# Projections of queries and keys on packed columns, placed by DMA, with a quarter of the adds on GpSimd

## The chip, the cores and the metric

The kernel runs on one NeuronCore of a Trainium2 chip. Its engines work side by side, each with a queue of its own: TensorE (PE, matmuls and transposes; PEld is its weight load), VectorE (DVE), ScalarE (ACT), GpSimd (POOL) and SyncE (SP, which here only issues DMAs). ACT and POOL can issue DMAs too. The metric is the device time of one execution in microseconds (us). A second, profiled execution gives the trace that the profile is read from.

## The reference

One transformer block in float32 on `x` of 4096 tokens by 256 features: a mixture of experts, attention, and the same mixture again.

```python
x = x + 0.5 * ffn(layernorm(x))
x = x + attention(layernorm(x))
x = x + 0.5 * ffn(layernorm(x))
```

`ffn` sends each token to 4 of 32 experts, adds their results with the routing weights, and adds a shared expert. `attention` has 16 heads of 16 features: `qkv = layernorm(x) @ qkv_w.T + qkv_b`, softmax of the scaled scores over all 4096 keys, times the values, and an output projection. The change concerns the adding up of the first mixture's results and the projections of queries and keys.

## The kernel before

**Order of the stages.** `first_front` normalizes and routes all tokens of the first mixture, clears the buffer `xg` and scatters the rows into it. `layer.experts` runs the experts and scatters their results into `ys`. `projections` adds up each token's results, normalizes, and makes queries, keys and values. `attention` runs scores, softmax and values, with the second mixture's front woven in; then come the second experts and a last loop that adds up and stores. The engines named in `ORDERED` (PE, ACT, DVE, SP) run the stage in the order of the program text; GpSimd's order is the framework's. DMAs issued on ACT or SP start in the order of those queues.

**Projections, block by block.** The stage has eight blocks (`NQB`) of 512 tokens (`QB`), four tiles of 128 each (`QT`). `fetch` loads the five rows of results per token of a tile, `y`, on SP; six such buffers exist, so a tile's load is asked for when the add of the tile six before it is done. `begin(c)` makes a block's rows:

- `add_up` (L763): per tile four DVE instructions (L765), each multiplying one expert's row by its weight `wk` and adding it to the sum; the first adds to the shared expert's row.
- `normalize` (L136): statistics (L141, L142) of the four tiles, an inverse root in some small steps (L144 to L157), then `xn` (L167), all on DVE.
- GpSimd adds the output projection's bias to `xt` (L910) and stores it to `x1` (L913) for attention.

A block's loop (L979 to L990) then goes: `turned` transposes the rows on PE (L177) and ACT copies them to `xT` (L180); `queries_or_keys(c, 0)`; `begin(c + 1)`, so that DVE makes the next block's rows meanwhile; `queries_or_keys(c, 1)`; `norms` of the queries; `values` (PE L961, DVE L969); `norms` of the keys; and a DVE reduction that sums `xT` over the block's tokens (L990).

**Layout of queries and keys.** Each head takes 32 rows (`HP`): 16 of data (`HD`), one row that is constant, and 15 rows of zeros. Four heads make one group of 128 rows, so 16 heads make four groups (`NG`). The weights `wqkv` come in this padded form, and each group costs one 128x512 product over two slices of the features (two matmuls at L922; the trace holds two records of each). ACT adds the bias twice per group: once as a plain copy (L935), into `kT` for keys and into a buffer `q` that ACT's queue stores to `qd` in DRAM for queries (L937), and once squared (L939). `norms` sums the squares by head with `of_head2`, four matmuls of 32 columns (L947), and DVE takes their maximum (L954).

**After the loop** the mean of the keys comes from the sums and the weights (L998 to L1025), then a bound on the scores and a shift for the queries (to L1044). A flag is read by all engines (L1343), and attention starts with a load of the first queries from `qd` (L1152).

**Loads at the stage's start** (L873 to L889), all on ACT's queue: `wqk_sb` (1 MB in pieces of 4 KB), `wv_sb` (two DMAs, in pieces of 64 bytes, one piece per head), `bv_sb` and `bproj_sb`.

Of the kernel before, what the change touches and what calls it, by code (L numbers as in the profile page):

```python
# [9 lines left out]
F32 = mybir.dt.float32  # L10
# [49 lines left out]
def kernel(  # L60
# [122 lines left out]
    class Layer:  # L183
# [573 lines left out]
        def finished(self, pool, t, xt):  # L757
# [2 lines left out]
            nc.sync.dma_start(y[:], by_token[:, t, :, :])  # L760
            self.add_up(y, t, xt)

        def add_up(self, y, t, xt):  # L763
            for k in range(K):
                nc.vector.scalar_tensor_tensor(  # L765
                    xt,
                    y[:, k, :],
                    self.wk[:, t, k : k + 1],
                    y[:, K, :] if k == 0 else xt,
                    ALU.mult,  # L770
                    ALU.add,
                )

    def first_front(layer, keep):
        n = layer.n
        with (
            tc.tile_pool(name="front", bufs=2) as pool,
            tc.tile_pool(name="ps_f", bufs=8, space=PSUM) as pm,
            tc.manual_schedule(engines=ORDERED),
        ):  # L780
            rows = 8
            zero = pool.tile([P, rows * RW], F32, name="zero", bufs=1)
            nc.vector.memset(zero[:], 0.0)
            nch = layer.nch
            xts = [
                pool.tile([P, n, D], F32, tag="x", name="xt", bufs=nch) for _ in range(nch)
            ]

            def load(ch, m):
                for i in range(0, n, m):  # L790
                    t = ch * n + i
                    nc.sync.dma_start(xts[ch][:, i : i + m, :], x_in[:, t : t + m, :])

            load(0, 2)
            load(1, n)


            xg = xgs[0]
            for e in range(E):
                nc.sync.dma_start(  # L800
                    xg[e * S0 + LOW : (e + 1) * S0, :].rearrange("(p r) d -> p (r d)", p=P),
                    zero[:, : (S0 - LOW) // P * RW],
                )
            for r in range(E * S0, CLEARED, rows * P):
                nc.sync.dma_start(
                    xg[r : r + rows * P, :].rearrange("(p r) d -> p (r d)", p=P), zero[:]
                )
            for ch in range(2, nch):
                load(ch, n)

            routes = [layer.route(ch, xts[ch], pool, pm) for ch in range(nch)]
            xTs = []

            def go_on(ch, pieces):
                for _ in range(pieces):
                    next(routes[ch])

            turns = NC * n // QT

            def norm(ch):  # L820
                go_on(ch, 2)
                xTs.append(layer.xT)

            def halves():
                for h in range(NT // QT):
                    ch, i = divmod(h, n // QT)
                    yield layer.shared_half(
                        xts[ch][:, i * QT : (i + 1) * QT, :],
                        xTs[ch][:, :, i * QB : (i + 1) * QB],
                        h * QT,  # L830
                        pool,
                        pm,
                    )

            half = halves()
            norm(0)
            go_on(0, turns)
            norm(1)
            for ch in range(nch):
                go_on(ch, 1)  # L840
                if ch + 1 < nch:
                    go_on(ch + 1, turns)
                go_on(ch, 2)
                between = next(half) if ch > 0 else iter(())
                next(between, None)
                go_on(ch, 3)
                next(between, None)
                if ch + 2 < nch:
                    norm(ch + 2)
                next(between, None)  # L850
            flag = layer.low(keep)

            late = iter(())
            for it in half:
                next(it)
                next(it)
                next(late, None)
                late = it
            next(late, None)
        return flag  # L860

    def projections(layer, side):
# [4 lines left out]
        with (  # L867
# [1 line left out]
            tc.tile_pool(name="ps_p", bufs=8, space=PSUM) as pm,  # L869
            tc.manual_schedule(engines=ORDERED),  # L870
        ):
            wqk_sb = pool.tile([P, NC, 2 * NG * P], F32, name="wqk_sb", bufs=1)
            nc.scalar.dma_start(  # L873
                wqk_sb[:], wqkv[:, : 2 * NG * P].rearrange("(c p) e -> p c e", p=P)
            )
            wv_sb = pool.tile([P, NC, NH, HD], F32, name="wv_sb", bufs=1)
            for c in range(NC):
                nc.scalar.dma_start(
# [20 lines left out]
            def begin(c):  # L899

                xt = pool.tile([P, QT, D], F32, tag="x", name="xt")
                for i in range(QT):
                    layer.add_up(ys_of.pop(c * QT + i), c * QT + i, xt[:, i, :])
                    if c * QT + i + 6 < NT:
                        ys_of[c * QT + i + 6] = fetch(c * QT + i + 6)
                xn = pool.tile([P, QT, D], F32, tag="xn", name="xn")
                rows = [xn[:, i, :] for i in range(QT)]
                for _ in normalize(pool, xt, rows, QT):
                    pass
                nc.gpsimd.tensor_tensor(  # L910
                    xt[:], xt[:], bproj_sb[:].unsqueeze(1).to_broadcast([P, QT, D]), ALU.add
                )
                nc.gpsimd.dma_start(x1_at[:, c * QT : (c + 1) * QT, :], xt[:])  # L913
                return rows

            def queries_or_keys(c, i, xT):

                squares = []
                for g in range(NG):
                    ps = pm.tile([P, QB], F32, tag="m", name="qk_ps")  # L920
                    for cc in range(NC):
                        nc.tensor.matmul(  # L922
                            ps[:],
                            wqk_sb[:, cc, (i * NG + g) * P : (i * NG + g + 1) * P],
                            xT[:, cc, :],
                            start=(cc == 0),
                            stop=(cc == NC - 1),
                        )
                    bias = bqk_sb[:, i * NG + g : i * NG + g + 1]
                    if i == 0:  # L930
                        q = pool.tile([P, QB], F32, tag="q", name="q", bufs=3)
                        part = q[:]
                    else:
                        part = kT[:, g, c * QB : (c + 1) * QB]
                    nc.scalar.activation(part, ps[:], AF.Identity, bias=bias)  # L935
                    if i == 0:
                        nc.scalar.dma_start(qd[c, g], part)  # L937
                    sq = pool.tile([P, QB], F32, tag="sq", name="sq", bufs=2 * NG - 1)
                    nc.scalar.activation(sq[:], ps[:], AF.Square, bias=bias)  # L939
                    squares.append(sq)  # L940
                return squares
# [1 line left out]
            def norms(c, i, squares):  # L943

                ps = pm.tile([P, QB], F32, tag="m", name="sq_ps")
                for g in range(NG):
                    nc.tensor.matmul(  # L947
                        ps[g * HP : (g + 1) * HP, :],
                        of_head2,
                        squares[g][:],  # L950
                        start=True,
                        stop=True,
                    )
# [24 lines left out]
            rows = begin(0)  # L978
            for c in range(NQB):  # L979
                xT = pool.tile([P, NC, QB], F32, tag="xT", name="xT")  # L980
                for _ in turned(pm, rows, QT, xT, nc.scalar.copy):
                    pass
                q2 = queries_or_keys(c, 0, xT)
                if c + 1 < NQB:
# [2 lines left out]
                norms(c, 0, q2)  # L987
                values(c, xT)
                norms(c, 1, k2)
                nc.vector.tensor_reduce(sums[:, :, c : c + 1], xT[:], AX.X, ALU.add)  # L990

# [6 lines left out]
            mean_in = small.tile([P, NC], F32, name="mean_in")  # L1000
            nc.vector.tensor_reduce(mean_in[:], sums[:], AX.X, ALU.add)
            nc.vector.tensor_scalar(mean_in[:], mean_in[:], 1.0 / T, None, ALU.mult)
            ps = pm.tile([P, NG], F32, tag="m", name="kmean_ps")
            for g in range(NG):
                for cc in range(NC):
                    nc.tensor.matmul(
                        ps[:, g : g + 1],
                        wqk_sb[:, cc, (NG + g) * P : (NG + g + 1) * P],
                        mean_in[:, cc : cc + 1],
                        start=(cc == 0),  # L1010
                        stop=(cc == NC - 1),
                    )
            mean = small.tile([P, NG], F32, name="mean")
            nc.vector.tensor_add(mean[:], ps[:], bqk_sb[:, NG:])
            nc.vector.tensor_mul(mean[:], mean[:], mean[:])
            ps = pm.tile([P, 1], F32, tag="m", name="mean_ps")
            for g in range(NG):
                nc.tensor.matmul(
                    ps[g * HP : (g + 1) * HP, :],
                    of_head2,  # L1020
                    mean[:, g : g + 1],
                    start=True,
                    stop=True,
                )
# [279 lines left out]
    for base, step, sign in ((0, -HP, 1), (HD - 1, HP, -1)):  # L1304
# [6 lines left out]
            base=base,  # L1311
            channel_multiplier=sign,
        )
    of_head2 = of_head[:].rearrange("p j r -> p (j r)")

    rows = const.tile([P, HG], F32, name="rows")
    nc.gpsimd.memset(rows[:], 1.0 / SCALE)
# [106 lines left out]
```

## Time and profile before

| What | us |
|---|---|
| Median of 3 runs (3371.22 to 3374.43) | 3372.26 |
| The profiled execution | 3374.66 |
| Span of its trace, first to last instruction | 3372.8 |
| TensorE busy in the span | 3072.7 (91%) |
| ScalarE busy | 2334.9 (69%) |
| VectorE busy | 975.3 (29%) |
| GpSimd busy | 616.0 (18%) |
| First load of results in the projections | 502.0 |
| First matmul of attention | 711.8 |

The page gives busy times over the whole span, a picture of the span in 40 slices, the DMA queues, the chain of work that ended last, and groups of instructions with what each waited for. Since the shares are means over stages with different limits, the stage that the change touches has to be read by itself: the timeline (start, length, engine, line, tile) and the busy time by stretches show which engine never rests there. A group's row reads: line, engine, operation, result and inputs, shapes, count, then busy us and mean ns of one, then the idle time before and what ended it.

### The profile page before, as it was taken

The page shows a single profiled execution, that of the slowest core. Times are in us where ns is not written, and L with a number is a line of the kernel's source. Part 1 is how long each engine was busy: PE and PEld are TensorE (multiplying, and loading weights), DVE is VectorE, ACT ScalarE, POOL GpSimd, SP SyncE. Part 2 cuts the span into 40 slices and gives each one's busy share as a digit, 9 for nine tenths or more (in the row PEclk, how much of TensorE's full clock was granted, in tenths as well). Part 3 has the DMA queues.
Part 4 walks back from the last instruction along what each step waited for, and adds up shares of the span by engine and source line. Part 5 has one row for each costly group of instructions (what it writes and reads, how often), then busy time and mean ns, then how long its engine had stood idle before and what let it go on. Part 6 is the DMA issues. An engine that isn't in the chain of part 4 may idle for free.

```text
span 3372.8 us, 50148 instructions
## 1 busy us (share of the span) xinstructions
PE 3072.7 (91%) x20183; PEld 1066.8 (32%) x20183; DVE 975.3 (29%) x2837; ACT 2334.9 (69%) x3753; POOL 616.0 (18%) x644
## 2 busy tenths in 40 slices
PE   4589977989999999999999999999999999959990
PEld 3356653422222222222222222222222222226660
DVE  6744437810112103201211210220121131044447
ACT  2112224569999898898999989889989998912220
POOL 2756661100001000100100010010010001025661
PEclk9799998989999999999999999999999999969995
DMA  6347756441300000000000010000000000017767
GB/s 236 118 182 244 247 189 242 153 135 56 100 4 20 26 7 4 27 20 4 30 20 4 13 33 4 7 27 20 4 30 20 4 6 31 1 64 238 254 204 315
DMA packets 130352, 282.20 MB, mean 84 GB/s; under 512 B 23472, under 2 KB 70192, under 8 KB 129712
## 3 DMA queue, kind: packets, MB, share of 16 engines
q1 hardware_dynamic: 82976, 165.84, 14.6%
q0 software_dynamic: 31872, 97.56, 7.9%
q10 hardware_dynamic: 15248, 15.38, 1.3%
q8 instruction: 163, 2.67, 0.3%
q14 instruction: 93, 0.76, 0.1%
HBM read 146.64 MB, written 132.06 MB: 83 GB/s over the span
## 4 chain that ended last, share of the span: by engine, by line
PE 70%; DVE 3%; issue 2%; DMA 2%; POOL 1%; ACT 0%; DVEq 0%; POOLq 0%; SPq 0%
PE banks L1170 33%; PE banks L1188 30%; PE banks L375 2%; DMA ys<-yb,toi 2%; PE h L718 2%; DVE xt L765 1%; POOL ys L748 1%; PE banks L1260 1%; PE banks L395 1%; PE o L740 1%; PE banks L233 1%; PE xbt_ps L692 0%; PE banks L177 0%; POOL wb L663 0%; DVE hT L729 0%
## 5 line engine op out<-in xcount | busy, mean ns | idle before, releaser
L1180 ACT ACTIVATE ex<-banks 128x512 f32<-128x512 f32 (+1 forms) x3223 | 2055.7, 714 | 164.7 <-PE banks L1170 129.1
L1170 PE MATMUL banks<-q,kT 32*128 32x512 f32 x8192 | 1177.6, 641 | 12.4 <-DVE q L1157 11.1
L1188 PE MATMUL banks<-ex,v 128*17 128x512 f32 x8192 | 1078.9, 598 | 0.0
L350 POOL DMA_INDIRECT xg<-xr,sidx x256 | 248.2, 969 | 2282.3 <-DVE beyond L343 2163.4
L1170 PEld LDWEIGHTS banks<-q,kT 32*128 32x128 f32 x8192 | 327.4, 183 | 847.4 <-ACT ex L1180 704.5
L1188 PEld LDWEIGHTS banks<-ex,v 128*17 128x17 f32 x8192 | 136.1, 95 | 777.5 <-issue 776.5
L1208 DVE COPY o<-banks 128x512 f32<-128x512 f32 x32 | 22.1, 691 | 1185.4 <-PE banks L1188 647.2
L748 POOL DMA_INDIRECT ys<-yb,toi x304 | 293.0, 964 | 177.3 <-DVE yb L746 94.8
L718 PE MATMUL h<-xT,w 128*128 128x512 f32 x512 | 236.0, 604 | 0.0
L744 ACT COPY yb<-o 128x512 f32<-128x512 f32 x64 | 37.5, 586 | 178.8 <-PE o L740 153.0
L740 PE MATMUL o<-w,hT 128*128 128x256 f32 x512 | 126.7, 392 | 34.2 <-DVE hT L729 34.2
L698 ACT COPY xT<-xbt_ps 128x512 f32<-128x512 f32 (+1 forms) x112 | 50.6, 452 | 126.4 <-PE xbt_ps L692 124.8
L727 ACT ACTIVATE s<-h 128x512 f32<-128x512 f32 (+1 forms) x112 | 51.5, 460 | 107.0 <-PE h L718 105.4
L718 PEld LDWEIGHTS h<-xT,w 128*128 128x128 f32 x512 | 95.2, 196 | 95.2 <-issue 95.2
L922 PE MATMUL qk_ps<-xT,wqk_sb 128*128 128x512 f32 x256 | 113.5, 602 | 1.7 <-ACT xT L180 1.7
L740 PEld LDWEIGHTS o<-w,hT 128*128 128x128 f32 x512 | 95.4, 194 | 55.1 <-DVE hT L729 36.9
L1211 DVE RECIPROCAL den<-den 128x512 f32<-128x512 f32 x32 | 107.3, 3353 | 1.1
L765 DVE SCALAR_TENSOR_TENSOR xt<-y,wk,xt 128x256 f32<-128x256 f32 x192 | 95.1, 495 | 6.9
L729 DVE TENSOR_TENSOR hT<-s,h 128x512 f32<-128x512 f32 (+1 forms) x112 | 57.8, 516 | 74.9 <-PE h L718 71.7
L375 PE MATMUL banks<-xT,ws_sb 128*128 128x512 f32 x128 | 68.9, 664 | 8.6 <-DVE u L385 6.5
L692 PE MATMUL xbt_ps<-ident,xb 128*128 128x128 f32 x512 | 69.6, 282 | 7.7 <-DMA xb<-xg 7.7
L443 PE MATMUL so<-ws_sb,shT 128*128 128x256 f32 x128 | 36.2, 441 | 43.5 <-DVE shT L437 28.9
(215 smaller groups left out, 1781.2 us busy)
## 6 DMA issues: line engine op xcount, KB each, us to landing
y<-ys SPq DMA_DIRECT2D x64, 640.0 KB, 6.9
xb<-xg SPq DMA_DIRECT2D x64, 528.0 KB, 5.7
w<-in_wexp_dram SPq DMA_DIRECT2D x64, 384.0 KB, 3.4
xg<-zeros SPq DMA_DIRECT2D x152, 132.0 KB, 2.3
xg<-zero SPq DMA_DIRECT2D x32, 264.0 KB, 4.3
qd<-q ACTq DMA_DIRECT2D x32, 256.0 KB, 5.5
q<-qd SPq DMA_DIRECT2D x32, 256.0 KB, 2.6
xbb<-xg SPq DMA_DIRECT2D x48, 132.0 KB, 3.7
```

Source lines behind the costliest of these rows:

```text
L350: ins = nc.gpsimd.indirect_dma_start(out=self.xg[:], out_offset=bass.IndirectOffsetOnAxis(ap=self.sidx[:, t0 + t, k : k + 1], axis=0), in_ ...
L375: nc.tensor.matmul(ps[:], ws13_sb[:, c, h0 : h0 + P], xT[:, c, i0 * P : (i0 + QT) * P], start=(c == 0), stop=(c == NC - 1),)
L692: nc.tensor.transpose(tp[:, i * P : (i + 1) * P], xb[:, i, c * P : (c + 1) * P], ident[:])
L718: nc.tensor.matmul(ps[:, : n * P], w[:, (j * NC + c) * H : (j * NC + c + 1) * H], xT[:, c, : n * P], start=(c == 0), stop=(c == NC - 1),)
L740: nc.tensor.matmul(o[:, i, :], hT[:, (i0 + i) * P : (i0 + i + 1) * P], w2, start=True, stop=True)
L748: ins = nc.gpsimd.indirect_dma_start(out=ys[:], out_offset=bass.IndirectOffsetOnAxis(ap=b["toi"][:, i : i + 1], axis=0), in_=yb[:, i, :], ...
L765: nc.vector.scalar_tensor_tensor(xt, y[:, k, :], self.wk[:, t, k : k + 1], y[:, K, :] if k == 0 else xt, ALU.mult, ALU.add,)
L922: nc.tensor.matmul(ps[:], wqk_sb[:, cc, (i * NG + g) * P : (i * NG + g + 1) * P], xT[:, cc, :], start=(cc == 0), stop=(cc == NC - 1),)
L1170: nc.tensor.matmul(pm.all[:, banks[j], :], kT[rows, g, t * P : (t + 1) * P], q[rows, :], start=True, stop=True,)
L1180: nc.scalar.activation(ex[:, i : i + n, :], pm.all[:, k : k + n, :], AF.Exp, scale=SCALE)
L1188: nc.tensor.matmul(acc[j * HP : j * HP + HV, :], v[:, t, g * HG + j, :], ex[:, j, :], start=(t == 0), stop=(t == NT - 1),)
L1211: nc.vector.reciprocal(den[:], den[:])
```

## The change

Two groups of heads share one set of 128 columns: the 16 rows that were padding for the first hold the second's data, so queries take two products instead of four, and keys likewise.

- **Weights.** `wqk_sb` is loaded by 16 DMAs on ACT's queue instead of one, each leaving out the padding (pieces of 64 bytes). The bias is brought to the same layout by six small DVE instructions.
- **Queries.** The padding rows of `qd` are cleared once, by 16 DMAs on SP in `first_front`, behind the loads of `x`. ACT adds the bias into a buffer `q`, and eight DMAs of 16 rows each, on SP, put its parts where attention expects them.
- **Keys.** ACT first fills the block's part of `kT` (the constant row and zeros), then eight DMAs per product place the 16-row parts in it, on SP too.
- **Squares and norms.** Two squares instead of four, and two matmuls of 64 columns with a new constant `of_half`, made by three GpSimd instructions. The mean of the keys follows the layout.
- **Sums.** ACT's copies to `xT` give the sums over tokens as they go; DVE's reduction L990 is dropped.
- **Adds.** The fourth tile of each block is added up on GpSimd by `add_up_aside`, four instructions; the other three stay on DVE. The last loop of the kernel keeps `add_up`.

```diff
+        def add_up_aside(self, y, t, xt):
+            w = self.wk[:, t, :].unsqueeze(2).to_broadcast([P, K, D])
+            nc.gpsimd.tensor_tensor(y[:, 0:K, :], y[:, 0:K, :], w, ALU.mult)
+            nc.gpsimd.tensor_tensor(y[:, 0:2, :], y[:, 0:2, :], y[:, 2:4, :], ALU.add)
+            nc.gpsimd.tensor_tensor(y[:, 0, :], y[:, 0, :], y[:, 1, :], ALU.add)
+            nc.gpsimd.tensor_tensor(xt, y[:, 0, :], y[:, K, :], ALU.add)
...
+            for g in range(NG):
+                for j in range(HG):
+                    nc.sync.dma_start(
+                        qd[:, g, j * HP + HD : (j + 1) * HP, :].rearrange("b r q -> r b q"),
+                        zero[:HP - HD, :QB].unsqueeze(1).to_broadcast([HP - HD, NQB, QB]),
+                    )
...
-            nc.scalar.dma_start(
-                wqk_sb[:], wqkv[:, : 2 * NG * P].rearrange("(c p) e -> p c e", p=P)
-            )
+            for cc in range(NC):
+                for a in range(2):
+                    for g in range(NG):
+                        h, i = divmod(g, 2)
+                        first_col = (a * NG + g) * P
+                        nc.scalar.dma_start(
+                            wqk_sb[:, cc, a, h].rearrange("p (j i d) -> p i j d", j=HG, i=2)[:, i],
+                            wqkv[
+                                cc * P : (cc + 1) * P, first_col : first_col + P
+                            ].rearrange("p (j r) -> p j r", j=HG)[:, :, :HD],
+                        )
...
-                    layer.add_up(ys_of.pop(c * QT + i), c * QT + i, xt[:, i, :])
+                    t = c * QT + i
+                    add = layer.add_up if i < QT - 1 else layer.add_up_aside
+                    add(ys_of.pop(t), t, xt[:, i, :])
...
+                cols = slice(c * QB, (c + 1) * QB)
+                if i == 1:
+                    nc.scalar.activation(
+                        kT[:, :, cols],
+                        zeros[:, 0:1].unsqueeze(2).to_broadcast([P, NG, QB]),
+                        AF.Identity,
+                        bias=one_row[:],
+                    )
                 squares = []
-                for g in range(NG):
+                for h in range(NG // 2):
...
-                            wqk_sb[:, cc, (i * NG + g) * P : (i * NG + g + 1) * P],
+                            wqk_sb[:, cc, i, h],
...
-                    nc.scalar.activation(part, ps[:], AF.Identity, bias=bias)
-                    if i == 0:
-                        nc.scalar.dma_start(qd[c, g], part)
-                    sq = pool.tile([P, QB], F32, tag="sq", name="sq", bufs=2 * NG - 1)
+                    bias = bias_sb[:, i, h : h + 1]
+                    part = pool.tile([P, QB], F32, tag="q", name="q", bufs=4)
+                    nc.scalar.activation(part[:], ps[:], AF.Identity, bias=bias)
+                    for r in range(0, P, HD):
+                        j, g = r // HP, 2 * h + r % HP // HD
+                        rows = slice(j * HP, j * HP + HD)
+                        if i == 0:
+                            nc.sync.dma_start(qd[c, g, rows, :], part[r : r + HD, :])
+                        else:
+                            nc.sync.dma_start(kT[rows, g, cols], part[r : r + HD, :])
+                    sq = pool.tile([P, QB], F32, tag="sq", name="sq", bufs=NG)
...
-                for g in range(NG):
+                for h in range(NG // 2):
                     nc.tensor.matmul(
-                        ps[g * HP : (g + 1) * HP, :],
-                        of_head2,
-                        squares[g][:],
+                        ps[h * 2 * HP : (h + 1) * 2 * HP, :],
+                        of_half,
+                        squares[h][:],
...
-                for _ in turned(pm, rows, QT, xT, nc.scalar.copy):
+                sums_of = iter([sums[:, cc, c : c + 1] for cc in range(NC)])
+                for _ in turned(
+                    pm,
+                    rows,
+                    QT,
+                    xT,
+                    lambda out, ps: nc.scalar.activation(
+                        out, ps, AF.Identity, accum_out=next(sums_of)
+                    ),
+                ):
...
-                nc.vector.tensor_reduce(sums[:, :, c : c + 1], xT[:], AX.X, ALU.add)
```

## The prediction

> **What bounds the kernel now.** I read the page from the top: the run without a profile and the profiled one agree (3372.26 us median of 3; 3374.66 us for the profiled execution, whose span is 3372.8, so 1.9 us lie around the span). The chain of work that ended last gives PE 70%, nearly all of it attention (L1170, L1188), which the change does not touch. So I went to the stage it does touch: the projections, from 502 us (the first load of results) to 711.8 us (the first attention matmul). First its costliest group on the page, then the timeline of one of its eight blocks, PE and DVE together:
>
> ```profile
> L922 PE MATMUL qk_ps<-xT,wqk_sb 128*128 128x512 f32 x256 | 113.5, 602 | 1.7 <-ACT xT L180 1.7
> ...
> 652.45 1.09 PE L177 MATMUL tp<-ident,xn 128*128 128x128 f32 x8
> 654.40 0.48 DVE L765 SCALAR_TENSOR_TENSOR xt<-y,wk 128x256 f32<-128x256 f32 x1
> 662.23 0.42 DVE L141 BATCH_NORM_STATS2 st<-xt 128x6 f32<-128x256 f32 x1
> 666.86 1.38 DVE L167 TENSOR_SCALAR xn<-xt,mv,r 128x256 f32<-128x256 f32 x4
> 673.35 1.09 PE L177 MATMUL tp<-ident,xn 128*128 128x128 f32 x8
> 674.68 14.00 PE L922 MATMUL qk_ps<-xT,wqk_sb 128*128 128x512 f32 x32 [0.24 <-ACT xT L180]
> 688.61 1.06 PE L947 MATMUL sq_ps<-sq,of_head 128*32 128x512 f32 x8
> 689.61 3.72 PE L961 MATMUL v_ps<-wv_sb,xT 128*128 128x256 f32 x16
> 693.26 1.06 PE L947 MATMUL sq_ps<-sq,of_head 128*32 128x512 f32 x8
> ```
>
> Columns: start us, length us. The reader is to see that PE never rests: transposes at 652.45 and again at 673.35, so a block takes **20.90 us**, and two thirds of it (674.68 to 688.61, 13.93 us) are the projections of queries and keys. Busy time by stretch says the same: from 553 to 576 us PE is busy 22.76 of 23.00. From the first transposes (524.78) to the last norms (693.26 + 1.06 = 694.32) the eight blocks take 169.5 us.
>
> **Projections halved.** The 32 matmul records of a block become 16: 13.93 / 2 = 6.97 us less, and PE's block is 20.90 - 6.97 = **13.9 us**. The norms go from four 32-column matmuls to two 64-column ones; if the pair runs side by side as the four do (1.06 us) nothing changes, if one after the other they are at most twice as long, 1.1 us each; the four are the nearest row, I take 0. What is late next is DVE.
>
> **DVE's block.** From the lines above: 16 adds take 662.23 - 654.40 = 7.83, so 0.489 each; twelve stay, 5.87. Statistics and roots 666.86 - 662.23 = 4.63; xn 1.38; two norm maxima of 0.69 and four value adds in two groups of 0.76, together 2.90. Sum 14.8 us; the sums of xT (1.21) are gone. All follow one another on DVE, so without collisions a block can't be under **14.8**.
>
> **GpSimd's four adds.** No such row stands there; the nearest is its one add of 128x1024, 2.35 us (L910). By size the four are 2.35 + 1.18 + 0.59 + 0.59 = 4.7; if an instruction costs the same at any size, 9.4. I take 4.7, since the largest is that row. (The Trainium skill, GPSIMD Engine Reference, section 3.1, gives 4497 ns for 2048 elements; with our 2.35 for 1024 this makes an estimate of 5.1.) Queue: L910, its store (0.77), then the four, with gaps of 0.3: 2.35 + 0.3 + 0.77 + 0.3 + 4.7 + 0.9 = 9.3 us after xn. DVE's statistics of the fourth tile wait for them, but are due only at 2.9 + 5.87 + 1.7 = 10.5: hidden, unless the two engines block each other. One place shows that they do, the first block, where L910 met DVE's adds:
>
> ```profile
> L765 DVE SCALAR_TENSOR_TENSOR xt<-y,wk,xt x4: 485/485/2452, 526.0 to 530.0; 128x256 f32<-128x256 f32 x4
> L910 POOL TENSOR_TENSOR xt<-xt,bproj_sb x1: 2359/2359/2359, 525.8 to 525.8; 128x1024 f32<-128x1024 f32 x1
> ```
>
> (min/median/max ns.) One add of 485 ns took 2452 while GpSimd's took its usual 2359: DVE lost 1.97 us, 83% of GpSimd's time. In the later blocks L910 runs beside a norm maximum, unhurt at 0.69. After the change the four adds start 3.7 us after xn, DVE's twelve 2.9 after it: they meet in every block. Loss 0.83 x 4.7 = 3.9, the block 14.8 + 3.9 = **18.7 us**. Bounds: no loss (14.8) and 0.83 x 9.4 = 7.8 (22.6).
>
> The Trainium skill (SBUF - State Buffer, "Who interferes with whom") speaks against this part: a DVE instruction with two SBUF inputs and a GpSimd one that reads SBUF exclude each other for a whole instruction. By it DVE would lose all 4.7 and the block be 19.5; without it 14.8. The row above sides with it.
>
> **ACT.** Eight of sixteen activations of 0.688 go (5.5 us); filling kT's block comes, 2048 elements. From 597 ns for 512 and 1029 for 1024 (L1180) that is about 1.9. ACT falls from 11.5 busy per block to about 8: hidden at 18.7, and nothing of it reaches the end. The copies' running sums cost between 0 and a second copy (0.59); hidden too, except in the last block; I take 0.
>
> **Placement by DMA, all on SP.** Per block 16 DMAs for queries, 4 loads of y, then 16 for keys, in this order. Issue: 36 x 0.32 (L894) = 11.5 us, up to 17.6 at the 0.488 that the slowest load of 16 partitions took (wproj, L129): covered by 18.7. But there is a chain. These lines of SP's own waits,
>
> ```profile
> SPq L894 <- DMA wqk_sb<-in_wqkv_dram: 9.7, 1, 9.7
> ...
> SPq L894 <- DMA bv_sb<-in_bv_dram: 3.1, 1, 3.1
> ```
>
> have no data behind them: y does not depend on wqk. At that point five loads on ACT's queue and three of y had gone out; the fourth y waited for the first of the eight to land. I read: eight DMAs in flight, the ninth waits for the first. So queries (16 x 0.32 = 5.1), y (1.3), the last y's landing (6.6 median), four keys held up by y (0.3), their landing (2.0), four more keys (1.3): 16.6 us a block, if a small DMA lands in under eight issues (2.6 us). That is below 18.7, so hidden; without the collision it would be the bound. The bytes stay: 256 KB x 4 of queries before, 2 x 512 KB now. Landing is bounded by the queries' store, 2.0 without and 5.5 us (median) beside the loads of y; I take 2.0, because y has landed when the keys go out.
>
> **Start.** Before: the fourth y lands at 517.52, the first transposes start at 524.78. Weights now come as 16 DMAs in 64-byte pieces. The rate of such pieces is wv's: 55 GB/s in the window 512 to 514. So 512 KB may take 9.5 us instead of 1 MB at about 380 GB/s, 2.8: between nothing (beside y, which itself no longer need wait: -4 at best) and +6.8; behind two rounds of wv's landing (11) it could be +12. I take +3.5. Then the fourth tile on GpSimd, 5.6 with gaps, plus its statistics 0.57, in place of 1.96 + 2.25: +2.0. Together **+5.5**.
>
> **End.** Without the sums 1.2; kmean's 16 records (3.24) halved, 1.6: **-2.8**. **Clock.** The granted clock is 0.50 from 510 to 530, where PE idles, and 1.00 after. PE would rest 4.8 us per block; in the last block, where PE is the bound again, I take +1 (0 to 2). (The Trainium skill, TensorE: Matmul & The Clock Gate, "What's actually happening", gives one idle window of about 3.4 us as enough; by it the last block would lose up to 1.7.)
>
> **Front.** 16 DMAs, 4.2 MB of zeros for qd, behind the loads of x on SP. DMA is full until 47 us, then idle (share 0.04 from 50 to 60), and SP's next store is much later; at 385 GB/s they take 11 us of that gap. Cost 0; at most 3 if they slow the scatters that start at 57.5. The extra constants on GpSimd are three instructions of about 0.25 us at 14 us, long before its first scatter.
>
> **Sum.** Seven blocks at 18.7 and a last at 13.9 are 144.8 against 169.5: -24.7. With +5.5, -2.8 and +1: **-21.0**. From 3374.66 that is 3353.7; the shown runs lie 2.4 lower, so **3351**.
>
> **Rivals.**
> 1. *The engines do not meet* (GpSimd's adds are put ahead of L910, or hardly block). Then the DMA chain bounds: 7 x 16.6 + 13.9 = 130.1, so -35.7: **3337**; at DVE's 14.8, 3324. For it: GpSimd idles 17.5 us per block before L910. Against: the 2452 ns.
> 2. *Small DMAs land late* (slower than before). If each round of eight waits for its landing r, the chain is four rounds and y: 4r + 6.6. At r = 5.5 it is 28.6: 7 x 28.6 + 13.9 = 214.1, +48: **3421**. It decides from 7P + 13.9 + 3.7 = 169.5, P = 21.7, r = 3.8. For: 5.5 in the page for qd, 5.3 for wproj. Against: 2.0 in the block at 653, where no y was loading. At r = 4.5: 3392.
> 3. *Gain eaten* (blocks of 20.7 to 22.7, as with GpSimd at 9.4): within 0.2%, which is about what a measurement can tell from no change, 6.7 us.
>
> **Chances.** Forecast 0.48 (blocks of 17.8 to 20.5, 3344 to 3364); rival 1 0.22; rival 3 0.08; rival 2 0.22. Faster 0.70, same 0.08, slower 0.22. The range reaches to 3326 (rival 1 almost at DVE's floor) and 3390 (r about 4.5).
>
> **What would show it.** Right: transposes 18 to 20 us apart; DVE adds above 1 us beside GpSimd's; PE idle at DVE's xn; qk at 6.9 us. Wrong: adds all at 0.49 and blocks of 17 or less; or SP's placements waiting on landings, with ACT waiting for q's buffers; or the first transposes later than 535.

## The result, and the profile after

| | us | ratio to before, 95% interval |
|---|---|---|
| before, median of 6 runs (3370.77 to 3379.77) | 3372.59 | |
| changed, median of 6 runs (3379.75 to 3393.57) | 3386.54 | 1.004 [1.0024, 1.0056] |
| changed, profiled execution (span 3378.0) | 3379.75 | |

The changed kernel is slower by 14 us. The forecast was 3351, faster by 21; its direction was wrong. (The stated range does reach to 3390, but by way of rival 2, not of the forecast's own working.) Line numbers from here on are those of the changed kernel.

I read the same stage again. First the group that answers to the one of before, from the groups of the stretch from 500 to 725 us (busy us, mean ns of one | idle time before):

```profile
L974 PE MATMUL qk_ps<-xT,wqk_sb 128*128 128x512 f32 x128 | 63.7, 655 | 2.6 <-ACT xT L1040 2.6
```

Half the records, 63.7 us instead of 113.5: PE does have less to do. Then one block, in the timeline (start us, length us):

```profile
607.36 8.30 SPq L988 DMA_DIRECT2D qd<-q  x16
...
611.95 1.97 PE L177 MATMUL tp<-ident,xn 128*128 128x128 f32 x8
...
613.84 8.26 PE L974 MATMUL qk_ps<-xT,wqk_sb 128*128 128x512 f32 x16
...
615.76 2.00 SPq L936 DMA_DIRECT2D y<-ys  x4
...
617.86 14.41 SPq L990 DMA_DIRECT2D kT<-q  x16
618.75 0.69 ACT L983 ACTIVATE q<-qk_ps,bias_sb 128x512 f32<-128x512 f32 x1 [0.50 <-ACT sq L992]
...
620.28 0.48 DVE L773 SCALAR_TENSOR_TENSOR xt<-y,wk 128x256 f32<-128x256 f32 x1 [3.62 <-DMA y<-ys]
620.80 3.27 DVE L773 SCALAR_TENSOR_TENSOR xt<-y,wk,xt 128x256 f32<-128x256 f32 x3
621.89 1.88 POOL L766 TENSOR_TENSOR y<-y,wk 128x1024 f32<-128x1024 f32 x1 [10.89 <-DMA y<-ys]
...
629.01 0.69 ACT L983 ACTIVATE q<-qk_ps,bias_sb 128x512 f32<-128x512 f32 x1 [7.11 <-DMA kT<-q]
...
632.38 1.91 SPq L988 DMA_DIRECT2D qd<-q  x4
```

Read the SPq lines alone: 8.30 + 2.00 + 14.41 us, each starting 0.1 us after the end of the one before, and at 632.38 the next block's queries begin (x4 because the view ends at 634). **SP's queue is never without work, and its round takes 25.0 us.** The other lines are late because of it. ACT waits 7.11 us at 629.01 for a buffer `q` that the placement has not yet emptied, and DVE waits 3.62 us for `y`, whose loads stood behind sixteen query placements.

Counted singly in the trace, a query placement (to DRAM) holds SP for 0.42 us, one each 0.46; a key placement (to SBUF) for 0.59, one each 0.63. Is it issuing or landing? These are the DMA issues of the stretch (KB each, median us from issue to landing) and SP's longest kind of wait in the blocks (us in total, times, longest):

```profile
qd<-q SPq DMA_DIRECT2D x128, 32.0 KB, 1.7
...
kT<-q SPq DMA_DIRECT2D x128, 32.0 KB, 2.0
```

```profile
SPq L990 <- DMA y<-ys: 22.4, 16, 2.8
```

The small DMAs land in the median within eight issues (8 x 0.46 = 3.7), and on SP they do not wait for each other. (The first key placements behind `y` do land late, the one at 617.86 after 9.15 us; `y`, sent ahead of them, is what the later ones wait for.) Only the larger loads of `y` (5.9 us) make the key placements wait, 22.4 / 8 = 2.8 us a block in the mean and 4.6 of the 14.41 us in the block shown. Sum: 16 x 0.46 + 2.0 + 16 x 0.63 + 2.8 = 22.2 us, of which 19.4 is issue.

The seven distances from one block's transposes to the next's are 19.4, 17.9, 25.9, 23.2, 25.3, 24.1 and 20.7 us, 156.5 together; before they were 23.1 and six of 20.9, 148.6. The stage ends with the same queue (last values, last placements, loads for attention, attention):

```profile
692.35 3.72 PE L1014 MATMUL v_ps<-wv_sb,xT 128*128 128x256 f32 x16
...
696.18 7.46 SPq L988 DMA_DIRECT2D qd<-q  x16
...
703.74 11.13 SPq L990 DMA_DIRECT2D kT<-q  x16
717.12 0.36 SPq L1213 DMA_DIRECT2D q<-qd  x1
717.60 0.38 SPq L1222 DMA_DIRECT2D xq<-x  x1
720.60 2.09 PE L1231 MATMUL banks<-q,kT 32*128 32x512 f32 x8 [16.66 <-DVE q L1218]
```

Attention starts at 720.6 instead of 711.8: +8.8. Attention itself adds 1.8 and what follows it gives back 5.4, which makes the 5.2 between the two spans (3378.0 and 3372.8); the profiled run is the fastest of its six. In a second profile of the changed kernel (span 3384.0) attention starts 7.1 later than before, 3.3 of which arose ahead of the stage, and attention and the rest add 4.1. The stage from its first load of `y` to attention is 218.1 and 213.6 us in the two, against 209.8: it accounts for 4 to 8 of the 14 us. The remainder is spread in pieces of a few us over stages whose code changed little or not at all, and no run here separates it.

### The profile page after: what moved, and what is told of

The parts are those of the page before. It is cut to its first block, busy times and chain, and to the rows that moved or that the text cites. A ratio compares the mean times of both kernels' runs of the same rounds, so it can differ in the third digit from the quotient of the medians.

```text
span 3378.0 us, 50147 instructions
## 1 busy us (share of the span) xinstructions
PE 3034.2 (90%) x19979; PEld 1045.9 (31%) x19979; DVE 954.4 (28%) x2803; ACT 2309.2 (68%) x3713; POOL 652.4 (19%) x679
## 4 chain that ended last, share of the span: by engine, by line
PE 69%; DVE 3%; issue 3%; POOL 2%; DMA 2%; ACT 0%; DVEq 0%; POOLq 0%; SPq 0%
PE banks L1231 33%; PE banks L1249 30%; POOL ys L748 2%; PE banks L375 2%; DMA ys<-yb,toi 2%; DVE xt L773 1%; PE banks L1321 1%; PE banks L395 1%; PE h L718 1%; PE o L740 1%; PE banks L233 1%; POOL wb L663 0%; PE banks L177 0%; PE xbt_ps L692 0%; PE banks L273 0%
## 5 line engine op out<-in xcount | busy, mean ns | idle before, releaser
L773 DVE SCALAR_TENSOR_TENSOR xt<-y,wk,xt 128x256 f32<-128x256 f32 x168 | 86.3, 514 | 6.0
L983 ACT ACTIVATE q<-qk_ps,bias_sb 128x512 f32<-128x512 f32 x32 | 22.0, 687 | 79.5 <-DMA kT<-q 41.4
L443 PE MATMUL so<-ws_sb,shT 128*128 128x256 f32 x128 | 36.0, 439 | 43.4 <-DVE shT L437 29.1
```

The costliest lines, as they stand in the source:

```text
L773: nc.vector.scalar_tensor_tensor(xt, y[:, k, :], self.wk[:, t, k : k + 1], y[:, K, :] if k == 0 else xt, ALU.mult, ALU.add,)
```

## The experiments

The runs were made on three chips, each with the kernel before beside them; it took 3577.72 us on chip A, 3372.51 on B and 3592.09 on C, so ratios to it on the same chip are compared. On A and C the changed kernel itself was not run. "Blocks" are the seven distances between transposes; "stage" is the time from the first transposes to the first matmul of attention.

| Run | Chip | Ratio, 95% interval | Blocks, us | Stage, us |
|---|---|---|---|---|
| before | | 1 | 23.1, then 20.9 | 187.0 |
| changed | | 1.004 [1.0024, 1.0056] | 17.9 to 25.9 | 195.0 |
| queries' placements on ACT | A | 1.0062 [1.0049, 1.0075] | 20.8 to 30.9 | 211.3 |
| all adds on DVE | A | 1.0016 [1.0004, 1.0027] | 18.7 to 27.3 | 200.1 |
| GpSimd's adds alone | A | 1.0011 [1.0001, 1.0021] | 22.5, then 20.9 | 185.6 |
| half of the parts placed | A | 0.9919 [0.9906, 0.9931] | 20.0, then 17.9 to 18.4 | 160.8 |
| changed, again | B | 1.0051 [1.0037, 1.0064] | 19.6 to 25.0 | 191.0 |
| half placed, adds on DVE | B | 0.9883 [0.9867, 0.9900] | 14.2 to 16.4 after 21.5 | 147.6 |
| short keys | B | 1.0035 [1.0022, 1.0047] | 17.9 to 24.1 | 190.7 |
| y on GpSimd's queue | B | 1.0001 [0.9992, 1.0011] | 15.9 to 22.3 | 173.7 |
| queries late on ACT | C | 1.0006 [0.9992, 1.0020] | 20.9 to 24.0 | 197.3 |
| keys to DRAM | C | 0.9958 [0.9940, 0.9976] | 17.6 to 22.9 | 173.7 |
| half placed, xn on ACT | C | 0.9893 [0.9874, 0.9912] | 17.0 after 17.5 and 15.1 | 147.6 |

**Theory I**: the time to issue 36 DMAs on one in-order queue sets the block. Its rivals: the DMAs' landing, bytes or number in flight (L), and the meeting of GpSimd and DVE (C). The expectations also use W (the DMA eight back must have landed) and B (bytes or landings), which are parts of L.

### Queries' placements on ACT's queue

```diff
-                            nc.sync.dma_start(qd[c, g, rows, :], part[r : r + HD, :])
+                            nc.scalar.dma_start(qd[c, g, rows, :], part[r : r + HD, :])
```

> The sixteen placements of queries per block are issued on ACT's queue instead of SP's; nothing else changes. Theory I (SP's issue time bounds a block: 16 x 0.46 + 4 x 0.5 + 16 x 0.63 and some 4 us of waiting on loads of y make the 24 us seen): SP falls to some 16 us a block, ACT rises from 8.3 busy to about 16, and the next bound is DVE with GpSimd's collisions, 17 to 19 us. About 35 us off the changed kernel: 3350, range 3340 to 3362. Theory C (GpSimd's adds and DVE's block each other, and the fourth tile comes late): nothing moves, 3380 to 3392. Theory W (the DMA eight back must have landed): the order of the loads is nearly the same, so blocks stay at 23 to 25 us, 3378 to 3392.

Ratio 1.0062: no gain, and theory I's number (3350 of 3372, a ratio of 0.993) missed. From the timeline of one block:

```profile
704.77 7.37 ACTq L988 DMA_DIRECT2D qd<-q  x8
...
712.18 0.69 ACT L992 ACTIVATE sq<-qk_ps,bias_sb 128x512 f32<-128x512 f32 x1 [7.45 <-DMA qd<-q]
...
723.61 9.99 SPq L990 DMA_DIRECT2D kT<-q  x16
```

ACT works through its instructions in order, issues among them. Its eight issues of a product stand ahead of the square at 712.18, which waits 7.45 us; such waits make 72.9 us between 625 and 800 us. Squares, fill and key parts are all behind them, so SP gets its first key part only at 723.61, 18.8 us after the queries' first placement. The queries' and the keys' placements follow one another and do not overlap. SP's sixteen keys, with y landed by then, take 9.99 us, 0.62 each: issue alone. The 7.37 us of ACT's eight are more than their issue, 8 x 0.47 = 3.8: its seventh and eighth start only at 709.88 and 711.83, when earlier DMAs have landed, and over the stage such waits of ACT's placements make 21.9 us in twelve places. So theory I named the resource rightly, but I had left out that ACT computes and must pay for issues in its own order; and waiting for landings, theory L's part, is not nothing in this run.

### All adds on DVE

```diff
-                    add = layer.add_up if i < QT - 1 else layer.add_up_aside
+                    add = layer.add_up
```

> GpSimd's quarter of the adds goes back to DVE; the placement stays as changed. Theory I: SP still needs 24 us a block, DVE 14.8 + 2 = 16.8 is hidden, so 3380 to 3390, no difference from the changed kernel beyond 5 us. Theory C: the blocks fall to 17 to 19 us, 3340 to 3355. Theory W: as I.

From the third on, blocks stay at 21.5 to 27.3 us, SP's waits for `y` too (25.7 us in the stage). GpSimd's adds do not set the changed kernel's block; theory C falls for it. The ratio, 1.0016, lies 0.0024 and 0.0035 (9 and 13 us) under the changed kernel's two, where theory I allowed 5 us; these were taken on another chip, and the stage is not shorter (200.1 us against 195.0 and 191.0), so the trace does not put this down to the blocks.

### GpSimd's adds alone

The kernel before with `add_up_aside` for the fourth tile (the same choice of `add` as in the diff of the change), and nothing else.

> The kernel before with one part of the change alone: the fourth tile's adds on GpSimd. PE needs 20.9 us a block there, DVE 16.8 - 2.0 + at most 4 of collisions = 18.8. Theory I: hidden except for the first block, 0 to +4 us on the kernel before: 3372 to 3377. Theory C: the fourth tile late on the path of every block, +1 to +3 us a block: 3380 to 3395.

Blocks 20.9, bounded by PE as before; ratio 1.0011. Where PE bounds, the adds cost little (4.6 us of 3578), and whatever they cost DVE in the blocks is covered.

### Half of the parts placed

ACT writes the first group of each product whole with a scale per row, 1 for its rows and 0 for the padding (the bias holds the constant row): into `kT` for keys, into a buffer with one store for queries. Only the second group is placed by DMAs, 10 + 4 + 8 per block instead of 36.

```diff
-                    for r in range(0, P, HD):
+                    nc.scalar.activation(
+                        first_group, ps[:], AF.Identity,
+                        bias=bqk_sb[:, a : a + 1], scale=low_half[:],
+                    )
+                    if i == 0:
+                        nc.sync.dma_start(qd[c, 2 * h], first_group)
+                    for r in range(HD, P, HP):
```

> Half of the placements go: the first of the two groups that share columns already lies in its rows, so ACT writes it whole (scaled by the mask of low halves, with the bias and the constant row), into kT for keys and into a buffer of its own for queries, which one DMA of 128 rows stores. Only the second group is placed by DMAs of 16 rows. SP issues 10 + 4 + 8 DMAs a block instead of 36; ACT has four activations of 0.69 more and a fill half as long. Theory I: SP 10 x 0.46 + 2 + 8 x 0.63 + 4 = 15.6 us, next bound DVE at 17 to 19: 3350, range 3338 to 3360. Theory C: unchanged, 3378 to 3392. Theory W: fewer rounds of eight, about 3.7 us off each of seven blocks: 3355 to 3368.

Blocks of 18.4 us and a ratio of 0.9919: with fewer issues, and ACT doing more, the change becomes a gain. This is the strongest evidence for theory I, since the matmuls, the adds and the layout are the changed kernel's. SP now has time to spare; its longest kind of wait from 660 to 770 us (us in total, times, longest) is for ACT's whole group:

```profile
SPq L998 <- ACT whole L990: 21.9, 5, 9.7
```

In the changed kernel SP's waits for ACT make 7.0 us in the stage, and DVE waits 62 us there: for norms, for the fourth tile and for `y`. Here DVE waits for nothing from 662 to 750 us. So DVE bounds, with the collisions that the prediction priced (timeline of one block):

```profile
702.58 5.13 DVE L773 SCALAR_TENSOR_TENSOR xt<-y,wk,xt 128x256 f32<-128x256 f32 x3
703.23 1.91 POOL L766 TENSOR_TENSOR y<-y,wk 128x1024 f32<-128x1024 f32 x1
705.22 1.34 POOL L767 TENSOR_TENSOR y<-y 128x512 f32<-128x512 f32 x1
...
706.63 0.79 POOL L768 TENSOR_TENSOR y<-y 128x256 f32<-128x256 f32 x1
707.50 0.79 POOL L769 TENSOR_TENSOR xt<-y 128x256 f32<-128x256 f32 x1
707.63 0.94 DVE L773 SCALAR_TENSOR_TENSOR xt<-y,wk 128x256 f32<-128x256 f32 x1
```

Three adds take 5.13 instead of 1.53, a fourth 0.94 instead of 0.48: DVE loses 4.06 us while GpSimd works for 4.83, 84%. The Trainium skill (SBUF — State Buffer, "Who interferes with whom") would have all of the 4.83 lost; the trace has most of it.

### The changed kernel again

> The changed kernel itself once more, as the measure for the three beside it: blocks of 23 to 26 us in the middle of the stage, ratio to the kernel before 1.002 to 1.006.

1.0051, which overlaps the first interval: the result holds.

### Half placed, and all adds on DVE

The two edits above together.

> As the kernel with half of the placements, but all adds on DVE. Where SP no longer bounds, theory C becomes the question. If GpSimd's adds and DVE's collide (3.6 us lost a block against 2.0 of work taken off), blocks fall from 18.4 to 16.8 and the kernel is 11 us faster than with half of the placements alone: ratio to the kernel before about 0.989. If SP still has a say (14 to 16 us of issue and waits) it is hidden just below. If the collision is no cost, blocks stay at 18.4 or grow to 20: ratio 0.992 to 0.996.

0.9883, faster than the kernel before and the changed one by more than the intervals: attention starts at 673.0 us, and blocks are 16.2 to 16.4 (15.8 and 14.2 near the start). Against the run with GpSimd's adds a block is 2.1 us shorter: the 4.06 lost in collisions, less 1.96 for the fourth tile's adds on DVE (4 x 0.489). So moving a quarter of the adds to GpSimd is itself a loss where DVE bounds. Busy time in a stretch as long as a block, 16.3 us:

```profile
606.30:622.60 16.30, 15.96 (x58) 8.66 (x57) 15.29 (x47) 10.13 (x18) 3.12 (x2) 1.00 0.75 257
```

(PE, PEld, DVE, ACT, POOL, granted clock, DMA share, GB/s.) DVE is busy 15.29 of 16.30 us, and it waits for nothing from 575 to 640 us: it bounds. PE's 15.96 is more than a block's work, since this stretch cuts across two blocks (58 records, where a block has 48); over three such stretches PE's mean is 15.05. The clock is back at 1.00 here.

### Short keys

```diff
-                            nc.sync.dma_start(kT[rows, g, cols], part[r : r + HD, :])
+                            nc.sync.dma_start(kT[rows, g, c * QB : c * QB + P], part[r : r + HD, :P])
```

> The changed kernel, but each of the keys' 128 placements moves 128 columns of 512; three quarters of the keys' data are left out (the filled zeros stay there). Theory I (a placement costs SP its issue time whatever it moves): still 0.63 a placement on SP and blocks of 23 to 26 us; ratio as the changed kernel within 0.2%. Theory B (the bytes or the landings bound): a quarter of the bytes, blocks of 20 or less, 15 us or more off.

Three quarters of the keys' data are left out. A quarter of the bytes, and nothing gained: 1.0035, and a key placement still holds SP for 0.59 us. From the DMA issues:

```profile
kT<-q SPq DMA_DIRECT2D x128, 8.0 KB, 1.8
```

Between 8 and 32 KB, bytes are not what is paid for; each DMA costs its issue. Theory L's part about bytes falls.

### y on GpSimd's queue

```diff
-                nc.sync.dma_start(y[:], by_token[:, t, :, :])
+                nc.gpsimd.dma_start(y[:], by_token[:, t, :, :])
```

> The changed kernel, but the loads of y go out on GpSimd's queue. SP is left with the 32 placements, 16 x 0.46 + 16 x 0.63 = 17.4 us, and none waits any longer for a y eight DMAs back. Theory I: blocks of 18 to 19.5 us (SP's 17.4 or DVE with collisions 18.4), 25 us off the changed kernel: ratio 0.993 to 0.998. If landings of the placements themselves bound, blocks stay above 22. GpSimd has 10 us of work a block and 3.2 of issues, so it should not bound, unless its queue holds y back behind its adds.

1.0001: the loss is back, and no more, where 0.993 to 0.998 was expected. No key placement waits for `y` any longer, blocks are 15.9 to 22.3 us (19.0 in the mean, as expected), and the stage from the first transposes on is 173.7 us instead of 195.0 and 191.0. Part of this is lost ahead, for the first transposes come at 536.4 instead of 525.6 and 527.9. The first load of `y` comes at 509.5 instead of 502.5 and 505.3, but at 509.7 with short keys too, where nothing was changed ahead of it; why the rest is lost, I have not settled. So `y` is a real share of SP's round, but without it SP's 17.4 us of placements still lie above PE's 13.9.

### Queries late on ACT

The queries' sixteen placements are issued on ACT's queue again, but after the block's last activation of keys, ahead of no key part.

```diff
+                for to, part in pending:
+                    nc.scalar.dma_start(to, part)
+                pending.clear()
```

> The changed kernel, but the queries' 16 placements of a block are issued on ACT's queue after the block's last activation of keys, so that they stand ahead of no key part. Theory I (time to issue on one in-order queue sets the block; the first try with ACT failed only because the issues stood ahead of the keys' activations): ACT's own work is about 8.3 us a block, 16 issues at 0.47 make 7.5, so ACT 15.8; SP keeps y (1.9), 16 key placements at 0.63 (10.1) and a wait of some 3 us for y, so about 15. Both lie under DVE's block with collisions (18.4, measured where only half of the parts were placed), so blocks of 18 to 19.5 us, and with the last block's placements at its end a ratio of 0.993 to 0.997 to the kernel before. Theory L (what counts is landing, or the number of DMAs in flight, whichever queue issues them): the same 36 DMAs take as long, blocks of 22 us or more, ratio 1.002 or more.

Neither theory's number: blocks of 22.5 us in the mean, as theory L had it (22 or more), with a ratio of 1.0006 between the two. (The profiled execution, 3608.03 us, is 15 us above this run's median, so its blocks may be longer than the usual.) The timeline of a block:

```profile
701.62 10.38 SPq L991 DMA_DIRECT2D kT<-q  x16
...
704.15 8.30 ACTq L1051 DMA_DIRECT2D qd<-q  x13
...
712.50 0.60 ACT L1041 ACTIVATE xT<-tp 128x512 f32<-128x512 f32 x1 [9.18 <-DMA qd<-q]
```

The issues now hold up the next block's first copy to `xT` instead (9.18 us at 712.50; the transposes had been done at 707.95), so they are still in the loop from PE over ACT back to PE. And they are dearer: 0.63 apart, the pace of SP's keys, where ACT alone had 0.47. The trace shows two things together. ACT's placements wait for DMAs to land, 26.1 us in seventeen places of the stage; and where they wait for nothing, as from 705.05 to 709.38, they hold ACT for 0.43 to 0.72 us each while SP issues too. SP, in turn, waits 66.4 us for ACT's `q`. So ACT bounds here by issue and landing both, and this run is no clean test of the two theories. It does show that ACT is no free place for issues.

### Keys to DRAM

```diff
-                            nc.sync.dma_start(kT[rows, g, cols], part[r : r + HD, :])
+                            nc.sync.dma_start(kd[c, g, rows, :], part[r : r + HD, :])
```

`kd` is a scratch array in DRAM; the keys' data are left out of `kT`, and attention works on the filled part alone, with the same instructions.

> The changed kernel, but the keys' placements write to a scratch array in DRAM instead of kT; left out: the keys' data never reach kT, so scores are computed from the constant row and zeros alone (attention's work is the same in size). This asks why one key placement takes 0.59 us to issue and a query placement 0.42. If the destination in SBUF is the reason: keys issue in 0.42, spaced 0.46, so 16 x 0.17 = 2.7 us less a block on SP, blocks of about 21 instead of 23.5, ratio 0.997 to 1.000. If it is their place in the queue (behind the loads of y, beside landing data): 0.59 stays, and the ratio is 1.003 to 1.006 as for the changed kernel.

A key placement now holds SP for 0.42 us, as a query's does: for these placements the destination in SBUF makes the 0.59. (It is not SBUF as such: the loads of `y` write SBUF too, and hold SP for 0.32 to 0.38.) The ratio, 0.9958, is lower than I expected: blocks are 20.0, 17.9, 17.6, 22.2, 22.9, 20.9 and 18.0 us. In the long ones the wait for `y` has remained (in one, sixteen key placements take 12.74 us where their issue alone makes 7.4); the short ones are at the 17.9 to 18.4 us at which DVE bounded above, and DVE waits for nothing in the first three.

### Half placed, xn on ACT

The step that makes `xn` is moved from DVE to ACT in the fastest version, after the block's keys.

```diff
-                for _ in normalize(pool, xt, rows, QT):
-                    pass
+                steps = normalize(pool, xt, rows, QT, on_act=True)
+                next(steps)
```

> The version with half of the parts placed by DMA and all adds on DVE (ratio 0.988, blocks of 16.3 us), with the step that makes xn from the statistics moved from DVE to ACT, four tiles at the end of ACT's work of a block. If DVE bounds that version (its busy time there, 16 adds, is 15.8 or more a block): 1.4 us less a block on DVE, so blocks of about 15 and, with seven of them, 8 to 10 us less, ratio 0.985 to 0.986. If SP's queue (10 query parts, 4 loads of y, 8 key parts and the wait for y) bounds it: blocks stay at 16.3, ratio 0.987 to 0.989. If ACT's added work (4 x 0.4) comes on the path instead: blocks of 17 or more and a ratio of 0.990 or more.

Blocks of 17.0 and 0.9893, no gain; the third outcome's numbers, nearly, but not its mechanism. The timeline shows a new collision:

```profile
698.53 2.34 POOL L958 TENSOR_TENSOR xt<-xt,bproj_sb 128x1024 f32<-128x1024 f32 x1 [13.57 <-ACT xn L163]
...
698.77 2.38 DVE L773 SCALAR_TENSOR_TENSOR xt<-y,wk 128x256 f32<-128x256 f32 x1
```

With `xn` later, GpSimd's bias add no longer runs beside a norm maximum but beside DVE's first add, which takes 2.38 instead of 0.48. 16.3 - 1.38 (`xn`) + 1.90 (the collision) + 0.16 (one small step more) makes 17.0. DVE did bound (it waits for nothing from 664 to 745 us), and the 1.38 was given back at once.

## Why the prediction was wrong, point by point

**The step that failed** is this one: "Issue: 36 x 0.32 (L894) = 11.5 us, up to 17.6 at the 0.488 that the slowest load of 16 partitions took (wproj, L129): covered by 18.7." In place of 0.32 the trace has 0.46 from one query placement to the next and 0.63 from one key placement to the next, 17.4 us for the 32 placements and 19.4 with the loads of `y`: over the 18.7, and over the upper bound too. I took the length of an isolated load on a queue with pauses for the pace of a queue without any. The kernel before did have a row for that pace, three loads of `y` issued back to back, 0.42 and 0.49 us apart:

```profile
513.08 1.27 SPq L894 DMA_DIRECT2D y<-ys  x3
```

Both loads in my rows also read from DRAM; the keys' way from SBUF to SBUF had no row at all, and I did not bound it upwards for that reason.

**The chain of eight in flight** was right in kind: small DMAs land in 1.7 to 2.0 us in the median and do not wait for each other on SP, only `y` makes the keys wait (the prediction's sequence). One reading was inexact: when the fourth `y` went out at 513.08, four of ACT's five loads had, and the fifth followed at 513.78; the count of eight comes out in the program's order only. But its sum of 16.6 was built on 0.32, and "hidden" fell with it: the measured round is 22 to 25 us.

**PE's block**: right. Sixteen records take 7.13 us where the clock is 1.00 (half placed, adds on DVE), and 8.26 in the block of the changed kernel shown, where PE rests and the granted clock is 0.81. The norms' pair takes 1.07: side by side, as taken.

**DVE's block and the collision**: right, where it can be seen. With half of the parts placed, blocks are 18.4 (18.7 foretold) and the loss 4.06 (3.9). In the changed kernel, against "they meet in every block", they meet in two of eight (five longer adds, 5.3 us in all), and SP's round covers it. GpSimd's quarter was not hidden there either: it gets its `y` late, and DVE waits 22.3 us in six blocks for the fourth tile. GpSimd's four instructions take 1.92 + 1.29 + 0.73 + 0.73 = 4.67 (4.7). The Trainium skill's page (GPSIMD Engine Reference, section 3.1) led to an estimate of 5.1, higher by 9%.

**ACT**: the fill takes 2.00 (1.9), a copy's sum 0.20 more; its own work was hidden, as said.

**Start**: +5.5 foretold; the first transposes came 0.8 later and the first projections 2.8. **End**: -2.8 and +1 and the shorter block foretold, 29.7 us from the last transposes to attention instead of 38.4; it stayed at 38.5, because attention's first load waits behind the last 32 placements (until 714.9). With half of them it is 31.1, and 30.9 with the adds on DVE too, so the working itself was sound to within 1.5 us. **Front**: a cost of 0, at most 3, was foretold for the sixteen clearing DMAs, with 11 us for their transfer. They keep SP's queue for 46.75 us (41.12 to 87.87), but its next store comes only at 109.1, and the first load of `y` at 502.5 instead of 502.0. Other runs scatter by several us (505.3 and 509.7 on chip B), so a cost of 1 or 2 us is not excluded.

**The sum of the misses** in the profiled stage: blocks 156.5 instead of 7 x 18.7 = 130.9, +25.6; end +8.8; start -5.3 (from the loads of `y` to the first transposes +0.2 instead of +5.5): +29.1 of the 29.3 between the foretold -21.0 and the measured +8.3 (first load of `y` to attention, 218.1 against 209.8). The rest of the measured +14, 6 us here and 10 in the second profile, lies outside the stage, and its cause stays open.

**Rivals.** Rival 2 had the right sign, the right queue and the right point of decision: the mean block is 156.5 / 7 = 22.4, above its 21.7. Its mechanism was wrong: it let each round of eight wait for a landing of 3.8 us or more, and landing takes 1.7 to 2.0 in the median; only the round behind `y` waits, 2.8 us a block. What lasts is the issue. Rival 1 had GpSimd and DVE free of each other; the collision of 84% refutes it. One of the marks that I had named as wrong did come: ACT waiting for `q`'s buffers (41.4 us for keys' placements in the stage).

A sentence of the Trainium skill (DMA: Bandwidth & Descriptors, "Issuing engines are not separate DMA queues") calls the time to start a DMA usually small relative to the DMA itself. Here one start is 0.42 or 0.59 of a landing of 1.7 or 2.0, and that rule alone would leave the block at 18.7; but starts add up on their queue, while landings overlap, and 32 starts make 17.4 us.

## What to carry to other kernels

Price a move "by DMA" as an instruction stream of its queue: number of DMAs times the spacing of back-to-back DMAs of that shape and destination, and compare it with the block that must cover it; bytes and landing came second here. Halving the number of placements, by letting an engine write whole what lies at its own partitions, turned a loss of 0.4 to 0.5% into a gain of 0.8%, and 1.2% with all adds on DVE. And work like these adds, moved to GpSimd, costs DVE most of GpSimd's time if they meet: 4.06 us lost to save 1.96.

## What the runs showed of the hardware that was not expected

- A DMA of 16 partitions out of SBUF holds SP for 0.42 us when it writes DRAM and 0.59 when it writes SBUF (the latter with 32 KB and with 8 KB alike); the loads of 128 partitions hold it for 0.32 to 0.38, all in the median.
- Two queues that issued at once kept a median pace of 0.63 us each, although one of them had 0.47 alone.
- GpSimd's multiplication of 128x1024 takes 1.92 us, where its addition of the same size (L954) takes 2.35.
- Where PE rested, its granted clock was lower: 0.78 to 0.83 in four blocks that SP bounds (PE busy 74 to 81%), 0.90 to 1.00 where DVE bounds (86 to 98%).
